# Sixteen transposed tiles instead of fifteen, and single tiles for the signs, in a four-layer graph network

## The chip, the cores and the metric

The kernel runs on one core of one Trainium2 chip. The time is the device time of the whole program in microseconds (us), from one launch. The names of the engines are those of the profile: PE is TensorE (matrix multiplication), DVE is VectorE, ACT is ScalarE, POOL is GpSimd, SP is SyncE, which here only issues DMAs. Each engine works through its own queue of instructions in a fixed order; semaphores hold an instruction back until what it needs is done.

## The reference

Sixteen graphs of 1024 nodes with 64 features each go through four layers. The adjacency matrix is symmetric in its pattern, but not in its values; about one entry in 128 is above zero, and the diagonal is. Each layer adds to `x` a function of `h = max(layernorm(x), 0)`.

```python
# layer 0
x = x + einsum('bnf,of->bno', einsum('bnm,bmf->bnf', adj, h), W0)
# layer 1: messages, and a GRU cell
m = relu(relu(h @ W1 + b1) @ W2 + b2)
msg = relu(einsum('bij,bjh->bih', adj, m))
r, z, n = gates(msg, h)                     # sigmoid, sigmoid, tanh
x = x + (1 - z) * n + z * h
# layer 2: Chebyshev, T0 = h, T1 = adj h, T2 = 2 adj T1 - T0
x = x + (K0 * T0 + K1 * T1 + K2 * T2) @ Wc + bc
# layer 3: quantiles over the neighbours that are left
nb = (adj > 0) without the diagonal; m = row count of nb
removed = every ceil(m / 2)-th neighbour of rows with m > 10, and its mirror image
agg = 0.25 * q25 + 0.5 * q50 + 0.25 * q75   # per node and feature, over self and neighbours
x = x + (relu((h + agg) @ M1 + c1) @ M2 + c2) * mask
```

So the adjacency matrix is multiplied four times per graph (once in layer 0, once in layer 1, twice in layer 2), and layer 3 needs a list of each node's neighbours and a sort of their features.

## The kernel before

**Tiles.** A graph's adjacency matrix is read as eight blocks of 128 columns (512 KB each, `block`, two buffers). PE transposes a block in eight pieces of 128x128, ACT copies the result from two PSUM banks into one tile `AT` of 128x1024 in fp32. There are `AT = 15` such tiles (line 106, taken into stock at line 602), eight for each graph. All four passes over the matrix of one graph read the same eight tiles, and the last pass of layer 2 gives tile after tile back (`into(..., last=True)` in `layers`), provided that the signs of this tile have been taken (`self.masked[b] > j`).

**Chains.** The work is written as Python generators that yield one operation at a time, or the name of a stock from which they want a buffer, or a condition to wait for. `transposing` loads and transposes blocks, graph after graph; it loads the block after the present one before it asks for the present one's `AT` tile. `layering` exists twice, for even and for odd graphs, and runs layers 0 to 2 (`layers`) for each, then the norm in front of layer 3; it ends with two stores by SP into DRAM, `table` (what is gathered) and `rows`. A graph's `X` (two buffers) may be loaded when the graph before has finished the matrix pass of layer 0 (`self.turns`), and its `pay` tile (three buffers) is taken at the end of layer 2. `coding` takes the signs of the transposed tiles, clears the diagonal and multiplies by a table of powers of two, so that sixty-three numbers per node (`words`, then `code`) tell which columns are set. `listing` turns a code into 24 column numbers per node, with DVE's largest-eight operations. `gathering` issues indirect DMAs from POOL, 80 for each graph (ten neighbours for eight tiles of nodes), and, after all graphs, 122 for nodes with more neighbours, which `longest` has picked out. `quantiling` sorts and weighs the gathered rows on DVE (`G`, two buffers, and `net`), and `dense` does the last two matrix products and stores the output.

**Order.** The class `Weave` plans the order of all engines' queues. It holds estimates of each operation's time and of each buffer's readiness, and always issues the operation that can start earliest by these estimates; among those within 0.1 us of each other on one engine it takes the lowest key. A graph's layers, transposes and codes have the key b − 3, its list b − 2, its quantiles and gathers b + 1. The written order is then fixed: on the chip an engine waits for the instruction at the head of its queue. All operations made through these chains have line 303 in the profile, so they are told apart by their tiles. Gathers are line 634, the stores of table, rows and output line 640.

**Around the change.** In `coding` (lines 664 to 694) two tiles of signs are held in one `there` tile of 128x2x1024 in fp16; there are two of these pairs. For each pair ACT takes two signs, DVE clears both diagonal blocks in one multiplication of 128x256, and PE does four multiplications, two for each tile. The result is scaled by ACT into the fp32 tile `words`, which has its own place, and is transposed by PE in four pieces.

Of the kernel before, what the change touches and what calls it, by code (L numbers as in the profile page):

```python
# [10 lines left out]
F32 = mybir.dt.float32  # L11
F16 = mybir.dt.float16
# [4 lines left out]
AF = mybir.ActivationFunctionType  # L17
# [5 lines left out]
P = 128  # L23
N = 1024
NT = N // P
C = 64
NB = 64
S = N // NB
# [74 lines left out]
RANK = 3.0  # L103
SHARE = 3
LONGEST = 512
AT = 15
XTILES = 2
PAYS = 3
LIST_KEY = -2
# [4 lines left out]
UNIT = 2.0 ** -10  # L114
# [213 lines left out]
class Weave:  # L328
# [13 lines left out]
    def stock(self, name, tiles):  # L342
        self.stocks[name] = list(tiles)

    def give(self, name, t):
        self.stocks[name].append(t)
# [121 lines left out]
class Fast:  # L468
# [4 lines left out]
    def __init__(self, tc, half, whole, weights):  # L473
# [107 lines left out]
        def stock(name, count, shape, dtype=F32):  # L581
            weave.stock(name, [p.tile(shape, dtype, name=f"{name}{i}") for i in range(count)])
# [6 lines left out]
        weave.stock("fm", banks[5:8])  # L589


        stock("there", 2, [P, 2, N], F16)
        stock("code", 1, [P, NT, NB])
        self.words = p.tile([P, 512], F32, name="words")
        self.top = p.tile([P, NT, WORDS], F32, name="top")
        self.cand = p.tile([P, NT, CAND], F16, name="cand")
        stock("L", 3, [P, NT, LIST], F16)
# [3 lines left out]
        stock("block", 2, [P, NT, P])  # L601
        stock("AT", AT, [P, N])
        stock("X", XTILES, [P, NT, C])
# [60 lines left out]
    def coding(self):  # L664

        V, T, S = self.V, self.T, self.S
        for b in range(GRAPHS):
            yield float(b) + CODE_KEY
            yield lambda: self.turns > 0
            bank = yield "bits"  # L670
            turned = self.turned[b]
            for j in range(0, NT, 2):
                there = yield "there"
                for i in range(2):
                    yield lambda: len(turned) > j + i
                    yield S.activation(there[:, i, :], turned[j + i], AF.Sign)
                self.masked[b] = j + 2
                own = there.rearrange("p i (t m) -> p (i t) m", m=P)[:, j:j + NT + 2:NT + 1, :]
                yield V.tensor_mul(own, own, self.noteye[:, None, :].to_broadcast([P, 2, P]))
                for i in range(2):  # L680
                    for half in range(2):
                        yield T.matmul(bank[half * NB:(half + 1) * NB, :], self.bits[:, (j + i) * NB:(j + i + 1) * NB],
                                       there[:, i, 512 * half:512 * half + 512], start=j + i == 0, stop=j + i == NT - 1)
                self.weave.give("there", there)
            yield S.activation(self.words, bank, AF.Identity, bias=self.low, scale=1.0 / UNIT)
            self.weave.give("bits", bank)
            bank = yield "tp"
            for q in range(4):
                yield T.transpose(bank[:, q * P:(q + 1) * P], self.words[:, q * P:(q + 1) * P], self.ident)
            code = yield "code"  # L690
            yield S.activation(code.rearrange("p (h q) w -> p q h w", h=2),
                               bank.rearrange("p (q h w) -> p q h w", h=2, w=NB), AF.Copy)
            self.weave.give("tp", bank)
            self.coded[b] = code
# [95 lines left out]
    def longest(self):  # L790
# [5 lines left out]
        for _ in range(3):  # L796
            tiles.append((yield "AT"))
        run = tiles[0][:, 0:BINS * Q]
# [59 lines left out]
        for t in tiled:  # L858
            self.weave.give("AT", t)


    def transposing(self, adj):
# [17 lines left out]
        for i in range(total):  # L880
# [4 lines left out]
            block = blocks.pop(i)  # L885
            at = yield "AT"
            for half in range(2):
# [39 lines left out]
    def layers(self, w, b, x):  # L927
# [9 lines left out]
        def into(bank, h, last=False):  # L937

            def step(j):
# [6 lines left out]
                if last:  # L946
                    yield lambda: self.masked[b] > j
                    give("AT", turned[j])
            return step
# [575 lines left out]
def general_layers(tc, b, x, adj, nodemask, VT, mB, X, H, maskT, c16, ident, ones16, ones_row, eps,  # L1525
# [3 lines left out]
    with tc.tile_pool(name="g1", bufs=1) as p1, tc.tile_pool(name="g2", bufs=2) as p2, \  # L1529
# [16 lines left out]
        def neighbours(g):  # L1546
            AT = p2.tile([P, NT, N], F32, name="AT")
            CN = p1.tile([P, NT, N], F16, name="CN")
# [434 lines left out]
```

## Time and profile before

| what | us |
|---|---|
| median of 13 runs | 2131.77 (2121.52 to 2144.62) |
| the profiled execution | 2133.97 |
| its span, from the first to the last instruction | 2132.0 |
| DVE busy | 1632.6 |
| PE busy | 1523.4 |
| POOL busy | 1432.9 |
| ACT busy | 1073.9 |
| granted clock of PE, mean over the span | 0.787 |

A line of the timeline gives the start in us from the span's start, the length in us, the engine, the line in the code, the operation with its tiles (out<-in) and form, how many of one kind are merged in the line (x), and in brackets how long the engine had been idle before and what ended this. A line of waits gives the waiting engine and tile, then what ended the wait, the sum in us, how often, and the longest. A line of the tile view gives the shortest, median and longest duration in ns, and the start of the first and of the last one in us. Idle time of an engine is a loss only where something later waits for it.

### The profile page before, as it was taken

The page shows a single profiled execution, that of the slowest core. Times are in us where ns is not written, and L with a number is a line of the kernel's source. Part 1 is how long each engine was busy: PE and PEld are TensorE (multiplying, and loading weights), DVE is VectorE, ACT ScalarE, POOL GpSimd, SP SyncE. Part 2 cuts the span into 40 slices and gives each one's busy share as a digit, 9 for nine tenths or more (in the row PEclk, how much of TensorE's full clock was granted, in tenths as well). Part 3 has the DMA queues.
Part 4 walks back from the last instruction along what each step waited for, and adds up shares of the span by engine and source line. Part 5 has one row for each costly group of instructions (what it writes and reads, how often), then busy time and mean ns, then how long its engine had stood idle before and what let it go on. Part 6 is the DMA issues. An engine that isn't in the chain of part 4 may idle for free. (4 is left out here: it accounts for less than half of the span.)

```text
span 2132.0 us, 22993 instructions
## 1 busy us (share of the span) xinstructions
PE 1523.4 (71%) x6172; PEld 713.3 (33%) x6172; DVE 1632.6 (77%) x4293; ACT 1073.9 (50%) x2921; POOL 1432.9 (67%) x1441
## 2 busy tenths in 40 slices
PE   6978677869787888788887878787978873233303
PEld 2443424333433343343433333334343331111202
DVE  2651587977788888888887969797788899949646
ACT  3654646556665657475656474747466532011000
POOL 2047776777576767677777667676757777776772
PEclk9979697978889787879796979787779886555555
DMA  4242626253525353434343353525252314121110
GB/s 122 70 86 57 117 36 96 61 96 61 92 61 88 68 75 80 66 89 62 84 67 89 49 94 61 106 51 95 51 92 51 43 31 42 30 32 23 32 27 11
DMA packets 246840, 140.93 MB, mean 66 GB/s; under 512 B 76048, under 2 KB 223952, under 8 KB 246704
## 3 DMA queue, kind: packets, MB, share of 16 engines
q1 hardware_dynamic: 195664, 88.11, 18.9%
q0 software_dynamic: 46096, 48.62, 17.3%
q10 hardware_dynamic: 4944, 2.66, 0.5%
q8 instruction: 53, 0.87, 0.2%
q14 instruction: 83, 0.68, 0.1%
HBM read 120.10 MB, written 19.17 MB: 65 GB/s over the span
## 5 line engine op out<-in xcount | busy, mean ns | idle before, releaser
L634 POOL DMA_INDIRECT G<-table,pay x1402 | 1403.2, 1001 | 652.8 <-issue 353.7
L303 PE MATMUL bank<-AT,nodes 128*64 128x512 f32 x2048 | 604.2, 669 | 87.1 <-ACT nodes L303 77.2
L303 PEld LDWEIGHTS bank<-AT,nodes 128*64 128x64 f32 x2048 | 181.2, 153 | 383.8 <-issue 221.7
L303 PE MATMUL bank<-G,c 128*128 128x512 f32 (+3 forms) x382 | 172.1, 589 | 184.8 <-DVE G L303 180.0
L303 PE MATMUL bank<-c,block 128*128 128x128 f32 x976 | 223.2, 349 | 102.2 <-DMA block<-in_adj 59.3
L303 ACT ACTIVATE AT<-bank 128x512 f32<-128x512 f32 x256 | 149.6, 589 | 187.2 <-PE bank L303 184.7
L303 PEld LDWEIGHTS bank<-c,block 128*128 128x128 f32 x976 | 147.8, 176 | 227.1 <-issue 143.4
L303 DVE TENSOR_TENSOR G<-G 128x512 f32<-128x512 f32 (+3 forms) x313 | 200.1, 673 | 2.8
L303 ACT ACTIVATE nodes<-X,off,ri 128x64 f32<-128x64 f32 x360 | 141.1, 429 | 45.9 <-DVE off L303 44.6
L303 DVE TENSOR_TENSOR net<-G 128x512 f32<-128x512 f32 (+6 forms) x240 | 150.6, 671 | 11.1 <-ACT G L303 9.1
L303 PEld LDWEIGHTS bank<-G,c 128*128 128x128 f32 x382 | 71.5, 224 | 255.8 <-DVE G L303 128.8
L303 ACT ACTIVATE G<-G,coef 128x64 f32<-128x64 f32 x384 | 98.2, 336 | 110.0 <-DVE coef L303 109.9
L303 ACT ACTIVATE sq<-X,st 128x64 f32<-128x64 f32 x360 | 124.6, 346 | 49.7 <-DVE st L303 33.4
L303 ACT ACTIVATE there<-AT 128x1024 f16<-128x1024 f32 x128 | 132.1, 1050 | 0.9
L303 ACT ACTIVATE wide<-bank 64x512 f32<-64x512 f32 x128 | 75.0, 586 | 109.3 <-PE bank L303 108.1
L303 DVE TENSOR_TENSOR G<-net 128x512 f32<-128x512 f32 (+7 forms) x189 | 117.1, 665 | 0.7
L303 DVE TENSOR_TENSOR G<-G,net 128x512 f32<-128x512 f32 (+3 forms) x177 | 111.3, 678 | 0.9
L303 DVE SCALAR_TENSOR_TENSOR G<-bad,G 128x512 f32<-128x512 f32 (+1 forms) x176 | 109.8, 692 | 0.0
L303 PE MATMUL bank<-wide,wg 64*64 64x512 f32 (+1 forms) x192 | 107.5, 642 | 0.9 <-ACT wide L303 0.4
L303 DVE TENSOR_REDUCE st<-X 128x8 f32<-128x512 f32 x48 | 32.9, 686 | 86.6 <-DMA X<-in_x 85.5
L303 DVE MAX8 L<-cand 128x8 f16<-128x103 f16 x384 | 91.9, 263 | 8.8
L303 PE MATMUL bank<-there,c 128*64 128x512 f16 x256 | 80.3, 450 | 25.4 <-DVE there L303 25.3
(200 smaller groups left out, 2225.8 us busy)
## 6 DMA issues: line engine op xcount, KB each, us to landing
block<-in_adj SPq DMA_DIRECT2D x121, 512.0 KB, 4.2
G<-table,pay POOLq DMA_INDIRECT x1402
rows<-pay SPq DMA_DIRECT2D x16, 632.0 KB, 10.4
table<-pay SPq DMA_DIRECT2D x16, 264.0 KB, 5.3
X<-in_x SPq DMA_DIRECT2D x16, 256.0 KB, 9.6
out<-yo SPq DMA_DIRECT2D x16, 256.0 KB, 2.6
G<-in_adj SPq DMA_DIRECT2D x3, 512.0 KB, 11.0
G<-in_adj ACTq DMA_DIRECT2D x3, 512.0 KB, 9.8
```

The costliest lines, as they stand in the source:

```text
L303: return Op(self, lambda: f(*args, **kwargs), writes, reads, cost, later)
L634: return self.nc.gpsimd.indirect_dma_start(out=out, out_offset=None, in_=table, in_offset=bass.IndirectOffsetOnAxis(ap=at, axis=0))
```

## The change

There are sixteen `AT` tiles. To make room, `there` becomes three single tiles of 128x1024 in place of two pairs, and the separate tile `words` goes: its values are written into a `there` tile, seen as 128x512 in fp32. The loop in `coding` runs over single tiles: one sign, one multiplication of 128x128 that clears the diagonal block, two matrix multiplications. `self.masked` counts tile by tile. In bytes per partition: one `AT` tile more is 4096, `there` goes from 8192 to 6144, and `words` gave 2048.

```diff
-AT = 15
+AT = 16
...
-        stock("there", 2, [P, 2, N], F16)
+        stock("there", 3, [P, N], F16)
         stock("code", 1, [P, NT, NB])
-        self.words = p.tile([P, 512], F32, name="words")
...
-            for j in range(0, NT, 2):
+            for j in range(NT):
                 there = yield "there"
-                for i in range(2):
-                    yield lambda: len(turned) > j + i
-                    yield S.activation(there[:, i, :], turned[j + i], AF.Sign)
-                self.masked[b] = j + 2
-                own = there.rearrange("p i (t m) -> p (i t) m", m=P)[:, j:j + NT + 2:NT + 1, :]
-                yield V.tensor_mul(own, own, self.noteye[:, None, :].to_broadcast([P, 2, P]))
-                for i in range(2):
-                    for half in range(2):
-                        yield T.matmul(bank[half * NB:(half + 1) * NB, :], self.bits[:, (j + i) * NB:(j + i + 1) * NB],
-                                       there[:, i, 512 * half:512 * half + 512], start=j + i == 0, stop=j + i == NT - 1)
+                yield lambda: len(turned) > j
+                yield S.activation(there, turned[j], AF.Sign)
+                self.masked[b] = j + 1
+                own = there[:, j * P:(j + 1) * P]
+                yield V.tensor_mul(own, own, self.noteye)
+                for half in range(2):
+                    yield T.matmul(bank[half * NB:(half + 1) * NB, :], self.bits[:, j * NB:(j + 1) * NB],
+                                   there[:, 512 * half:512 * half + 512], start=j == 0, stop=j == NT - 1)
                 self.weave.give("there", there)
-            yield S.activation(self.words, bank, AF.Identity, bias=self.low, scale=1.0 / UNIT)
+            there = yield "there"
+            words = there.bitcast(F32)
+            yield S.activation(words, bank, AF.Identity, bias=self.low, scale=1.0 / UNIT)
             self.weave.give("bits", bank)
             bank = yield "tp"
             for q in range(4):
-                yield T.transpose(bank[:, q * P:(q + 1) * P], self.words[:, q * P:(q + 1) * P], self.ident)
+                yield T.transpose(bank[:, q * P:(q + 1) * P], words[:, q * P:(q + 1) * P], self.ident)
+            self.weave.give("there", there)
```

## The prediction

> **What bounds the kernel now.** I read the page first, then one tile's instructions (the stores of the table), then what each engine waited for, and last the timelines of ACT, PE, DVE, SP and POOL around one turn of the steady state, 560 to 690 us, where graph 5 ends and graph 6 is under way. The run behind the profile took 2133.97 us, 1.97 more than its span; the median of the runs shown is 2131.77, so the sum below is made against 2134 and taken down by 2.2 at the end.
>
> ```profile
> span 2132.0 us, 22993 instructions
> PE 1523.4 (71%) x6172; PEld 713.3 (33%) x6172; DVE 1632.6 (77%) x4293; ACT 1073.9 (50%) x2921; POOL 1432.9 (67%) x1441
> ```
>
> No engine is full over the span. The steady part is a chain of sixteen graphs, and its step is read from the table stores, one per graph; what POOL (which gathers, and whose last gathers set the end) waits for is the second view.
>
> ```profile
> L640 SPq DMA_DIRECT2D table<-pay x16: 359/366/367, 125.1 to 1770.9; - x16
> ...
> POOL G L634 <- DVE whole L303: 37.9, 5, 13.9
> POOL G L634 <- DMA table<-pay: 31.9, 6, 13.9
> POOL G L634 <- DVE below L303: 19.8, 2, 14.2
> POOL G L634 <- DVE st L303: 8.2, 1, 8.2
> ```
>
> Fifteen steps in 1645.8 us are 109.7 us a graph. The four lines add to 97.8 us. They stand at the starts of graphs' gathers, and the names whole, below and st are only what ended last: each time the gather starts about 6 us after that graph's table store (563.14 and 569.58, 672.94 and 679.56 below). So POOL is short of work by 6.5 us per graph on the mean. Its sixteen stretches of 80 gathers, cut out of the timeline, are 1674 us in sum, 104.6 each: that is the floor under the step if the stores came early.
>
> What makes the store late is seen in one turn. Two chains of layers are in flight, one for even and one for odd graphs, and graph 6 cannot finish layer 0 without its eighth transposed tile.
>
> ```profile
> 623.73 0.58 ACT L303 ACTIVATE AT<-bank 128x512 f32<-128x512 f32 x1
> ...
> 656.09 0.60 ACT L303 ACTIVATE AT<-bank 128x512 f32<-128x512 f32 x1 [9.99 <-PE bank L303]
> ```
> ```profile
> 563.14 0.37 SPq L640 DMA_DIRECT2D table<-pay  x1
> ...
> 672.94 0.37 SPq L640 DMA_DIRECT2D table<-pay  x1
> ...
> 673.99 1.01 SPq L303 DMA_DIRECT2D X<-in_x  x1
> ```
> ```profile
> 569.58 0.94 POOL L634 DMA_INDIRECT G<-table,pay  x1 [14.23 <-DVE below L303]
> ...
> 679.56 0.94 POOL L634 DMA_INDIRECT G<-table,pay  x1 [5.52 <-DVE below L303]
> ```
> ```profile
> 655.99 1.07 PE L303 MATMUL bank<-AT,nodes 128*64 128x512 f32 x2
> ...
> 672.88 2.00 PE L303 MATMUL bank<-w0t,wide 64*128 64x64 f32 x16
> ```
> ```profile
> 676.01 0.67 DVE L303 TENSOR_TENSOR X<-X,bank 128x512 f32<-128x512 f32 x1
> ...
> 684.03 0.69 DVE L303 TENSOR_REDUCE st<-X 128x8 f32<-128x512 f32 x1 [5.24 <-DMA X<-in_x]
> ```
>
> Seven tiles of graph 6 are turned by 624.3; the eighth starts at 656.1, when graph 5's last pass gives its first tile back: fifteen tiles are eight for graph 5 and seven for graph 6. Its block had been asked for at 621.9, in the same timeline of SP. From 656.1 to the sum of layer 0 (676.7) are 20.6 us, and these lie behind graph 5's last pass and in front of graph 6's layer 1. The step is therefore a closed loop: last pass of one graph, eighth tile, layer 0's end, then layers 1 and 2 up to the next last pass. That it is latency and not load shows between the first two stores (125 to 224 us, 99.0 us), where DVE is busy for 37.6 and PE for 74.6.
>
> **The change, part by part.** *The sixteenth tile.* It takes the eighth tile out of the loop: graph 6's could be turned 31.8 us earlier (656.1 less 624.3) and its layer 1 may start while graph 5 is in layer 2. Tiles are then wanted again only by graph 7's first transposes, which have a whole step. Nothing is added: the same 1024 transposes, 256 copies and block loads, moved earlier. Past SP: the eighth load of a graph and, because a graph's X may be asked for once the one before has finished layer 0, the X load can be queued in front of the table store, not behind it; its issue is 1.0 us in the row above, which the store may bear once a graph (15 us in all at most, and less than nothing if X lands earlier). Past POOL nothing moves: it issues gathers in graph order alone.
>
> What is late next. POOL allows 104.6 a graph. DVE is busy 91.5, 92.0, 93.2 and 90.5 us in the four steps from 563 to 1001 (mean 91.8), and in a step of the same length it waits some 16 us: over 673 to 1673, nine graphs, 48.1 us for X, 27.6 for the root of the norm, 24.0 for the candidates' relu, that is 11.1 a graph, and about 5 a graph for smaller waits. With the 0.8 us below, 91.8 + 0.8 + 11.1 is 103.7, under POOL's floor; with the smaller waits kept it is 108.7. The second graph in layer 1 gives DVE and PE other work in front of these waits, but each queue runs in one written order and the waits of a chain do not vanish. I take the middle of POOL's floor and that sum, (104.6 + 108.7) / 2 = 106.7, as nothing in the trace says which is nearer: 3.0 us a graph, 15 times, **−45 us**. Ends: −97.8 (all of POOL's waits at starts go) and 0 or worse (the third case below).
>
> *The first graph.* Graph 0's last passes, 99 to 125 us, now share PE and ACT with graph 1's eighth tile and layer 1. Eight transposes of 0.33 us and two copies of 0.6 are 3.8 us in front of the first store: **+4 us**, since POOL's row begins there. Bounds: nothing if they fall into the 25 us of PE's idle time of that stage, 12 if one pass of graph 1's layer 1 goes first as well (8.29 us for the 32 instructions in the timeline at 708).
>
> *Signs one by one.* The activations stay 128 of 1050 ns. The masking multiply is done 128 times over 128 columns, not 64 times over 256 (287 ns). The new size has no row; 192 columns take 258 and 72 take 235, so I take 245: 8 x 0.245 less 4 x 0.287 is 0.8 us of DVE a graph, 13 us in all, with 0.7 and 0.9 as ends from those rows. It is hidden in DVE's 16 us of waits a graph; were that cover gone, it would be 13 us on the end. A sign's order is finer: behind it on ACT are copies and relus, and the multiply now comes one sign (1.05 us) earlier for the first of each pair; gain or loss at most that per pair, off the loop, because the list it feeds is wanted some 50 us later. With three singles a sign waits for the multiplication three signs back (two pairs: the third or fourth back). In the trace ACT is idle for 0.9 us in front of all 128 signs, so a buffer wait costs nothing now, and nothing up to 1 us each on ACT's 42 us of idle time.
>
> The VectorE: DVE Perf Modes page of the Trainium skill (§ Rules for kernel authors) says to keep the number of operations small, and its errata section puts some 150 cycles on each one whatever its size. By that estimate the 64 added multiplies cost 64 x 0.156 us, 10 us, all of it against the change; the rows above give a little more.
>
> *Words in a `there` tile.* The activation (680 ns) and four transposes stay. They hold one of three tiles for about 4 us (663.35 to 664.75 in this turn at the least), after the graph's last sign, and the next graph's first sign comes 10 us or more later: nothing, and 16 x 4 us at worst on a chain with 50 us to spare.
>
> Sum: 2134 − 45 + 4 = 2093, less 2.2, and I say **2091 us**.
>
> **The rivals.** *Nothing to gain.* The loop is cut, but the step stays with DVE's order: 91.8 + 0.8 busy and its waits as they are make 108.7 to 109.7. Or graph 1's X tile (two of them) or the pay tile (three) takes the wait over: a pay tile comes back with its graph's output store (630.79 in this turn, for graph 2) and graph 5's is taken at 658.0, so that there are 27 us of room, a little less than the 31.8 the loop gives. For it: DVE is over 82% busy in each steady step. Against: the step of 99 us without DVE load. Price: 0 to 1 us a graph, 2117 to 2136.
>
> *Slower.* Two graphs in layers at once fill DVE's queue with two sets of short dependent operations (norms of 0.17 to 0.7 us, each with a wait on ACT in the middle). The order is written by a planner whose times are estimates: X's load lands after 9.6 us by the profile, where DVE stands waiting today. If such waits come to stand in front of the other graph's final norm, they are on the way to the store. Place: DVE between two stores. It decides at 109.7 − 92.6 = 17.1 us of DVE waiting a graph, against 16 now; at 20 us the step is 112.6, +2.9, and 15 steps give +44: 2176. For it: margin is one microsecond. Against: DVE would have more work ready to stand in front of a wait, not less.
>
> *The change does not do what it says.* The eighth block may not be there, or the order may put its transposes behind layer 2 all the same. The block is asked for at 621.9 and PE waits 5 us at 630 to 635, so little speaks for it; it would give 2132 and up to 13 for the multiplies. I count it with the first rival.
>
> **How the numbers follow.** The forecast gets 0.55, nothing to gain 0.15, slower 0.30. A difference of 0.3%, about 6.4 us, is what a measurement of this kernel can tell from none. Of the 0.15, 0.05 lies below 2125, 0.08 within and 0.02 above. Faster is 0.60, same 0.08, slower 0.32. The forecast's own range is 2034 (all 97.8 us) to 2120. The whole range goes from 2034 to 2160: below it are waits that I don't see, above it the slower case's far half; together 2 in 10.
>
> The SBUF — State Buffer page of the Trainium skill (§ Who interferes with whom) states that a DVE operation with two SBUF inputs can hold up a GpSimd one that reads SBUF. The 64 added multiplies are such operations; if each held a gather for its own length, an estimate by that page is 64 x 0.245, 16 us more on POOL. The trace's gathers have a median of 944 ns beside a mean of 1001, which shows that some are held, not by whom.
>
> **What would show it.** In the changed profile: graph b+1's sixteenth copy no longer waits for graph b's last pass, and its layer-0 sum is done 20 us or more before graph b's store. POOL's waits at the starts fall from 97.8 us to about 50, the stores' step to 106.7, and the first store is at 129. The `there` multiply has 128 instructions near 245 ns. The prediction is wrong if the step stays at 109 or more: then DVE's waits per graph will be 16 us or more, and that row tells the first rival from the second. The tail after graph 15's gathers should keep its length, 237 us from 1895 to 2132; if it grows, the lists or the quantiles are behind POOL there.

## The result: 2.1% slower, and the profile after

The changed kernel takes 2178.01 us (median of 14 runs, 2159.6 to 2192.2) against 2130.86 us before (62 runs beside it, 2119.9 to 2146.3): 1.021 of the time, 95% interval 1.019 to 1.0231. (This and the ratios below are those on record, which go by the fast runs alone; quotients of the two medians differ from them by up to 0.2%.) The forecast was 2091 us with a range up to 2160. Both missed, and the sign was wrong.

The page of the changed kernel, its head:

```profile
span 2181.0 us, 23079 instructions
PE 1548.0 (71%) x6172; PEld 715.7 (33%) x6172; DVE 1635.8 (75%) x4357; ACT 1079.3 (49%) x2921; POOL 1425.8 (65%) x1441
```

The 64 added multiplies raised DVE's busy time by 3.2 us only, and POOL and ACT do what they did. The span is 49 us longer all the same, so the time is in waits. The span falls into four pieces, read from POOL's timeline: the time up to the first gather, the sixteen stretches in which a graph is gathered, the idle time between two stretches, and the tail behind graph 15's last gather.

| us | before | after | difference |
|---|---|---|---|
| up to the first gather | 130.4 | 139.8 | +9.4 |
| sixteen stretches | 1666.3 | 1698.6 | +32.3 |
| between them | 98.0 | 105.9 | +7.9 |
| tail | 237.3 | 236.7 | −0.6 |
| span | 2132.0 | 2181.0 | +49.0 |

The largest piece is the one that the prediction had treated as a fixed floor. The table's stores and POOL's waits after the change (a group row of the stores, then engine, tile, what the wait ended on, us in all, times, longest):

```profile
L639 SPq DMA_DIRECT2D table<-pay x16: 359/366/367, 134.3 to 1806.2; - x16
...
POOL G L633 <- DMA table<-pay: 123.1, 1, 123.1
POOL G L633 <- DVE net L303: 59.9, 3, 28.8
POOL G L633 <- PE bank L303: 59.8, 42, 17.4
```

Two of these waits as they were before:

```profile
POOL G L634 <- PE bank L303: 12.1, 30, 3.2
...
POOL G L634 <- DVE net L303: 9.9, 1, 9.9
```

(The 123.1 us are the wait in front of the very first gather.) The stores' step is (1806.2 − 134.3) / 15 = 111.5 us, 1.8 longer than before. "DVE net" has gone from 9.9 to 59.9 us and "PE bank" from 12.1 to 59.8. (Of the 59.9, 50.7 are two waits in front of graphs 7 and 14; the third, like the 9.9 before, lies in the tail.) Both are waits for a gather buffer G: net is the sorting network that reads G, and the bank is filled from G by the last matmuls that use it. Inside stretches POOL stood idle for 40.7 us (waits above 1 us, less the usual 0.3), against 2.2 before. The wait for a graph's own store is no longer the only one.

The turn that the prediction looked at, graph 6's layer 0, in the changed kernel. Timelines of ACT, SP, PE and DVE:

```profile
592.00 0.58 ACT L303 ACTIVATE AT<-bank 128x512 f32<-128x512 f32 x1
...
630.67 0.59 ACT L303 ACTIVATE AT<-bank 128x512 f32<-128x512 f32 x1
...
677.33 0.60 ACT L303 ACTIVATE AT<-bank 128x512 f32<-128x512 f32 x1 [0.39 <-PE bank L303]
```
```profile
576.96 0.37 SPq L639 DMA_DIRECT2D table<-pay  x1
...
687.38 0.37 SPq L639 DMA_DIRECT2D table<-pay  x1
```
```profile
582.36 0.42 PE L303 MATMUL bank<-c,nodes 128*64 128x128 f32 x1 [15.14 <-ACT nodes L303]
...
666.68 3.65 PE L303 MATMUL bank<-AT,nodes 128*64 128x512 f32 x16 [0.26 <-DVE nodes L303]
...
672.81 0.66 PE L303 MATMUL bank<-c,block 128*128 128x128 f32 x4
```
```profile
698.15 0.67 DVE L303 TENSOR_TENSOR X<-X,bank 128x512 f32<-128x512 f32 x1
```

With sixteen tiles the eighth need not wait for graph 5's last pass. In this turn it comes behind it all the same: the second half of that pass ends on PE at 670.3, the eighth tile's transposes start at 672.8, and its copies are at 673.5 and 677.3, 10 us before graph 5's store at 687.4 (15 us before). The other tiles are late as well. Six copies, three tiles, are done by 592.6; then none comes for 38 us, and the sum of layer 0 ends at 698.8, 11.4 us after graph 5's store, where before it was 3.8 us after the store. The written order has put the transposes of graph 6 behind other work (PE does graph 5's layers and the last products of a quantile from 594 to 629), and PE stood still for 15.1 us around the start of that turn.

This turn is the worst of fifteen. Before, the sixteenth copy of the next graph starts 11.3 to 12.0 us after the first operand of a graph's last pass is ready, in every turn; after the change it starts 11 to 27 us ahead of that in eleven turns and 4 to 15 behind it in four. So the tile does come earlier in most. But the sum of layer 0 does not follow: on the mean of the fifteen turns it ends 4.3 us behind the previous graph's store before and 3.6 after, and from the sixteenth copy to the matmuls of this sum (graphs 4 to 14) it takes 12 to 17 us before and 17 to 47 after.

### The profile page after: what moved, and what is told of

It reads as the page before. It is cut to its first block, busy times and chain, and to the rows that moved or that the text cites. A ratio compares the mean times of both kernels' runs of the same rounds, so it can differ in the third digit from the quotient of the medians.

```text
span 2181.0 us, 23079 instructions
## 1 busy us (share of the span) xinstructions
PE 1548.0 (71%) x6172; PEld 715.7 (33%) x6172; DVE 1635.8 (75%) x4357; ACT 1079.3 (49%) x2921; POOL 1425.8 (65%) x1441
## 5 line engine op out<-in xcount | busy, mean ns | idle before, releaser
L303 PE MATMUL bank<-AT,nodes 128*64 128x512 f32 x2048 | 592.7, 662 | 49.0 <-ACT nodes L303 37.3
L303 PE MATMUL bank<-G,c 128*128 128x512 f32 (+3 forms) x382 | 198.6, 651 | 204.3 <-DVE G L303 166.4
L303 PEld LDWEIGHTS bank<-AT,nodes 128*64 128x64 f32 x2048 | 173.5, 150 | 356.0 <-issue 209.4
L303 ACT ACTIVATE there<-AT 128x1024 f16<-128x1024 f32 x128 | 134.3, 1050 | 1.0
L303 PE MATMUL bank<-c,nodes 128*64 128x128 f32 x128 | 50.7, 407 | 90.7 <-ACT nodes L303 89.5
L303 PE MATMUL bank<-wide,wg 64*64 64x512 f32 (+1 forms) x192 | 103.1, 618 | 2.3 <-ACT wide L303 2.1
```

The source lines that it names most:

```text
L303: return Op(self, lambda: f(*args, **kwargs), writes, reads, cost, later)
```

## Experiments

Every batch ran beside the kernel before on the same chip, and chips differ by up to 1%: before took 2130.86 us beside the changed kernel, 2126.82 in the first batch (e1 to e4), 2111.91 in the second (e5 to e8), 2111.55 in the third (e9 to e12), 2110.55 in the fourth (e13 to e16). So ratios are compared. In the table, "inside" is POOL's idle time within stretches, "starts" that in front of them, whether for the store or for G (both less 0.3 us a gather), and "half clock" the sum of those stretches of the trace's clock record that begin between 40 and 1700 us and grant PE half its speed. The last five columns are of one profiled execution each, not divided by the kernel before of the same batch: e5, in the order of before and 1.0005 of its time, has a step of 108.2 us on its chip, against 109.7. A profiled execution can also lie off its median: e2's is the fastest of ten (2109.89 us, median 2128.19), e7's the slowest of ten (2117.4, median 2108.55).

| run | ratio to before, 95% | first store | stores' step | starts | inside | half clock |
|---|---|---|---|---|---|---|
| before | 1 | 125.1 | 109.7 | 93.5 | 2.2 | 570 |
| after | 1.021 (1.019–1.0231) | 134.3 | 111.5 | 101.4 | 40.7 | 659 |
| e1 signs alone | 1.0183 (1.0149–1.0216) | 133.2 | 111.5 | 112.3 | 6.5 | 614 |
| e2 tile alone | 1.0006 (0.997–1.0042) | 125.8 | 108.0 | 47.6 | 18.3 | 539 |
| e3 after, lists later | 1.0157 (1.0122–1.0192) | 133.1 | 110.1 | 43.8 | 56.5 | 597 |
| e4 before, lists later | 1.0059 (1.0028–1.009) | 125.5 | 109.3 | 59.8 | 38.0 | 526 |
| e5 singles, order of before | 1.0005 (0.9981–1.0029) | 126.1 | 108.2 | 76.3 | 0.8 | 567 |
| e6 after, PE filled | 1.010 (1.0055–1.0145) | 126.9 | 108.4 | 62.9 | 31.0 | 430 |
| e7 before, PE filled | 0.9978 (0.9962–0.9994) | 129.4 | 108.3 | 81.6 | 0.7 | 413 |
| e8 tile alone, filled | 0.9966 (0.9931–1.0001) | 124.0 | 106.8 | 35.6 | 16.7 | 389 |
| e9 signs alone, filled | 1.0045 (1.0012–1.0078) | 124.7 | 109.2 | 71.3 | 5.4 | 437 |
| e10 e6 and lists later | 1.0069 (1.0038–1.0099) | 126.4 | 108.8 | 18.6 | 63.0 | 451 |
| e11 e8 filled more | 0.9946 (0.992–0.9972) | 125.7 | 107.5 | 46.3 | 22.4 | 362 |
| e12 e11, lists later | 1.0078 (1.0051–1.0104) | 132.4 | 108.6 | 69.6 | 18.3 | 440 |
| e13 after, lists apart | 0.9976 (0.9955–0.9998) | 133.5 | 107.5 | 56.4 | 5.6 | 536 |
| e14 e13 filled | 0.9896 (0.9864–0.9928) | 129.9 | 107.2 | 48.1 | 9.3 | 429 |
| e15 e11, lists apart | 0.9853 (0.9821–0.9885) | 125.3 | 106.3 | 18.8 | 21.0 | 348 |
| e16 after, start filled | 1.0188 (1.0157–1.022) | 128.6 | 109.8 | 87.7 | 30.6 | 611 |

### Which part of the change costs (e1, e2)

e1 is the change without its first line: single-tile signs, words in one of them, fifteen tiles. Against the changed kernel:

```diff
-AT = 16
+AT = 15
```

> The signs part alone: fifteen transposed tiles, three single tiles of signs, words in one of them. Theory A (what costs is the written order of DVE's queue: a list of neighbours, 80 or more operations and some 30 us, is put inside a quantile, so that the gather buffer G comes back late and POOL stands): in the written order of this kernel a whole list stands inside the quantiles of graphs 5 and 6, where the kernel before has none inside those of graphs 1 to 12 and the changed one has one inside 2, 5, 7 and 12. So two long waits of POOL, 15 to 30 us each, behind graphs 7 and 8, and 2150 to 2165. Theory B (the sixteenth tile costs, by bringing two graphs' layers into each other's way): the time of before plus no more than the 13 us of small multiplies, 2130 to 2145, with no long wait of POOL inside a graph's gathers.

e2 is the first line alone. So that sixteen tiles fit beside the pairs, the words go into a pair of signs and the scratch of the lists into an output tile:

```diff
-AT = 15
+AT = 16
-        self.words = p.tile([P, 512], F32, name="words")
-        self.top = p.tile([P, NT, WORDS], F32, name="top")
+            there = yield "there"
+            words = there[:, 0, :].bitcast(F32)
...
+        lent = yield "yo"
+        top = lent[:, 0:NT * WORDS].rearrange("p (t w) -> p t w", w=WORDS)
```

> The sixteenth tile alone: pairs of signs as before; the room comes from writing words into a pair of signs and the list's scratch tile top into an output tile. Theory A: in the written order a whole list stands inside the quantiles of graphs 2, 4 and 10, so three waits of POOL of 6 to 25 us behind graphs 4, 6 and 12 and 2145 to 2175. Theory B: all of the loss, 2170 to 2185, and spread over all graphs. If the tile takes the eighth transposition out of the loop as I forecast, the time would be below before, 2091.

The signs alone cost 1.8%, the tile alone nothing that can be measured. The prediction had it the other way round: 45 us of gain for the tile, nothing for the signs. In e1 the loss stands mostly at starts: in front of graph 7 alone POOL waits for 36.8 us, until 933.3, 42 us behind that graph's store at 891.2. What ends this wait is "DVE net", with a list inside graph 5's quantile, as Theory A said; e1's 2163.03 us lie in its range.

e2's 2128.19 us lie in none of the three ranges. Lists stand inside the quantiles of graphs 2, 4 and 10, and POOL's waits behind graphs 4, 6 and 12 came as Theory A said (12.2, 16.5 and 10.5 us), all three for G, but the time did not rise. So a list inside a quantile makes POOL wait, but what such a wait costs depends on the rest of the order.

### Lists half a graph later (e3, e4)

```diff
-LIST_KEY = -2
+LIST_KEY = -1.5
```

The key is the priority with which the planner takes up a graph's list. Why lists came under suspicion is seen on DVE in the changed kernel. This is the quantile of graph 5 (hits is its first operation, the operations on G and net its network):

```profile
834.57 0.32 DVE L303 TENSOR_TENSOR hits<-G,pay 128x160 f32<-128x160 f32 x1 [0.21 <-DMA G<-table,pay]
...
881.90 0.42 DVE L303 TENSOR_SCALAR top<-code 128x504 int32<-128x504 int32 x1
...
889.04 0.69 DVE L303 TENSOR_TENSOR G<-net,G 128x512 f32<-128x512 f32 x1
...
903.64 0.67 DVE L303 TENSOR_TENSOR G<-net,G 128x512 f32<-128x512 f32 x1
```
```profile
904.58 0.99 POOL L633 DMA_INDIRECT G<-table,pay  x1 [0.30 <-issue]
927.45 1.15 POOL L633 DMA_INDIRECT G<-table,pay  x1 [21.88 <-DVE net L303]
```

From 881.9 to 910.7 the list of graph 8 runs, and the network gets single operations in between. From the first operation to the last this quantile takes 97 us, where the others of graphs 1 to 11 with less than 4 us of a list inside take 66 to 71. There are two gather buffers; graph 7 needs the one that graph 5's quantile still reads, and POOL stands for 21.9 us, until 20 us behind graph 7's store at 907.4, where some 6 are usual. Before, the quantiles of graphs 1 to 12 hold no list. After, those of 0, 2, 5, 7 and 12 hold 23 to 29 us of DVE's work on one, and the long waits for G are exactly in graphs 2, 4, 7, 9 and 14.

> The changed kernel with one number changed: the key of the lists is b - 1.5, not b - 2, so that the quantile of graph b - 3 goes before the list of graph b where both can start. Theory A: G comes back in time again, POOL's waits of over 5 us inside a graph's gathers go, its waits on DVE net and PE bank (119.7 us in the changed kernel) fall below 40, and the time falls by 50 to 70 us, to 2110 to 2130, at or under the kernel before. Theory B: the layers of two graphs still share the queues, so that not more than 15 us come back: 2163 or more.

> The kernel before (fifteen tiles, pairs) with the same one number changed. Theory A: it has no list in front of a quantile's operations to begin with, so nothing is to be won: 2125 to 2160, as the list now comes later than the eighth tile's wait allows. If the key alone were a gain whatever the number of tiles, it would be 2080 to 2110. Theory B says nothing of it.

The later key helps the changed kernel by half a per cent, far less than expected, and costs the kernel before as much. The traces tell why: with the later key the quantiles of graphs 1 to 13 have a list inside in both kernels, and in the changed kernel the waits at starts fall to 44 and those inside rise to 57. This was the wrong tool for the question, not an answer to it.

### The instructions or their order (e5)

The kernel before, with each pair's two signs in two tiles and its multiply done as two, while the planner goes on reckoning with one of the old cost. So every engine's written order is that of before, one multiply more per pair apart (and a few operations behind the last graph's list).

```diff
-                own = there.rearrange("p i (t m) -> p (i t) m", m=P)[:, j:j + NT + 2:NT + 1, :]
-                yield V.tensor_mul(own, own, self.noteye[:, None, :].to_broadcast([P, 2, P]))
+                yield self.each_own(there, j)
...
+    def each_own(self, there, j):
+        own = [there[i][:, (j + i) * P:(j + i + 1) * P] for i in range(2)]
+        def make():
...
+        return Op(self.V, make, own, own, 0.155 + 2 * P / 960)
```

> The kernel before with each pair of signs put into two separate tiles and the pair's one masking multiply (128x256) done as two (128x128), one behind the other; every engine's written order is otherwise that of before, instruction by instruction, and fifteen transposed tiles are kept. Theory I (the finer instructions themselves cost: 64 more operations on DVE, smaller tiles): most of the 36 us that the single-tile signs cost at fifteen tiles comes back here, 2145 to 2163 us, first store near 133. Theory O (the written order costs, not the instructions): 2121 to 2135 us, first store at 125 as before, DVE's busy time up by 3 to 10 us and hidden in its waits.

The group of multiplies there (min/median/max ns, first and last start):

```profile
L702 DVE TENSOR_TENSOR there<-there,c x128: 204/217/285, 46.9 to 1637.5; 128x128 f16<-128x128 f16 x128
```

1.0005. The same 128 small multiplies that e1 has cost nothing in the order of before. Theory O holds: the 1.8% come with the order that the planner writes once the signs are single. Nor is it a lack of tiles: planned with four single tiles in place of three, the kernel of e1 has the same written order, instruction by instruction.

### PE at half clock (e6 to e9, e16)

What else differs is seen in the first graph. Stretches of the timeline, first before, then after. The columns are the stretch and its length, the busy time and the number of instructions of PE, PEld, DVE, ACT and POOL, then the granted clock, the DMA share and GB/s:

```profile
52.00:56.00 4.00, 4.00 (x16) 2.00 (x15) 2.70 (x6) 4.00 (x7) 0.00 (x0) 0.62 0.44 128
56.00:60.00 4.00, 3.01 (x21) 1.98 (x21) 1.23 (x4) 3.94 (x13) 0.00 (x0) 1.00 0.47 136
60.00:64.00 4.00, 3.96 (x19) 1.71 (x18) 2.69 (x10) 4.00 (x11) 0.00 (x0) 1.00 0.01 2
```
```profile
52.00:56.00 4.00, 1.99 (x9) 0.94 (x10) 3.50 (x9) 3.99 (x9) 0.00 (x0) 0.95 0.59 167
56.00:60.00 4.00, 4.00 (x13) 1.66 (x12) 0.85 (x4) 3.05 (x6) 0.00 (x0) 0.50 0.29 88
60.00:64.00 4.00, 4.00 (x9) 0.91 (x10) 0.00 (x0) 1.67 (x3) 0.00 (x0) 0.50 0.01 2
...
72.00:76.00 4.00, 4.00 (x14) 1.70 (x15) 2.44 (x14) 2.01 (x9) 0.00 (x0) 0.50 0.01 4
```

After the change PE has work for only 2 of the 4 us from 52 on. Then its clock is 0.50 from 55.6 to 76.1, 20.5 us in which PE is busy nearly all the time. Before, the same place has two windows of 3.4 us at half clock (from 51.7 and from 65.3). This goes with the first store's delay, 125.1 to 134.3: e1 and e3, which have the order of the single signs, show the same 20.5 us and 133; e2 and e5, which haven't, show neither. Whether it is the cause, filling PE's idle time tells.

The filling puts matmuls that do no work in front of an operation before which the planner foresees PE idle. They write ones where that operation will overwrite, or add zeros to what is being summed. The order stays as it is, and the planner doesn't reckon with them:

```diff
+IDLE, FILL, WARM = 0.8, 0.7, (5.0, 1720.0)
...
-        line, ins = op.line, op.make()
+        line = op.line
+        gap = start - self.free.get(line, 0.0)
+        if op.fill and self.last.get(line) and gap > IDLE and WARM[0] < start < WARM[1]:
+            each, fill = op.fill
+            for _ in range(min(40, int(FILL * gap / each))):
+                ins = fill()
...
+        ins = op.make()
```

> The changed kernel, every engine's written order kept, with idle stretches of PE that the written order foresees (over 0.8 us) filled to about 70% with matmuls that do no work: they write ones into a region that the next matmul overwrites, or add zeros to one that is being summed. Theory C (PE at half clock is what the new order costs: in the profiles PE ran at half clock for 658 us between 40 and 1700 us in the changed kernel, 614 with the single-tile signs alone, 570 before, 539 with the sixteenth tile alone): half-clock time falls under 500 us and the time by 20 to 45 us against 2178, to 2133 to 2158; the first store comes at 127 or earlier, because the 20 us at half clock from 55 to 76 us go. Theory W (the order's waits on DVE and ACT cost, and the clock only follows): 2170 to 2190, also where the half-clock time falls.

> The kernel before with the same filling of PE's foreseen idle stretches. Theory C: half-clock time between 40 and 1700 us falls from 570 to under 480 us and the time by 10 to 30 us, to 2097 to 2117. Theory W: 2120 to 2140 us, with the filling matmuls in front of real ones costing 0 to 12 us.

> The sixteenth tile alone with signs in pairs (the kernel of the second experiment, 2128 us), with the same filling of PE's foreseen idle stretches. Theory C: 2095 to 2118 us, faster than the kernel before. Theory W: 2122 to 2140.

The same stretches in e6, where PE does 10 instructions more from 52 to 56:

```profile
52.00:56.00 4.00, 2.85 (x19) 1.29 (x19) 3.26 (x9) 3.99 (x9) 0.00 (x0) 1.00 0.57 168
56.00:60.00 4.00, 4.00 (x18) 1.57 (x17) 0.85 (x4) 3.73 (x8) 0.00 (x0) 1.00 0.24 70
60.00:64.00 4.00, 4.00 (x24) 2.35 (x22) 0.81 (x3) 3.73 (x9) 0.00 (x0) 1.00 0.21 63
```

With 812 matmuls that compute nothing the changed kernel loses half of its deficit, 1.021 to 1.010, and its first store comes 7.4 us earlier. The stores' step falls from 111.5 to 108.4; some 1 us of that is the chip's (e5 above). The kernel before gains only 0.2% by the same means, though its half-clock time falls by 157 us (570 to 413), and Theory C's 10 to 30 us did not come there. So time at half clock has no fixed price. It should count where others wait for PE, but beyond the first graph no run shows which stretches these are. e8's interval just touches 1 and is inconclusive by itself.

> The single-tile signs alone at fifteen tiles (1.0183 of before in the first experiment) with PE's foreseen idle stretches filled as in the sixth. If half-clock time is what this part of the change costs, it comes to 0.995 to 1.004 of the kernel before, with the first store at 127 or earlier and the stores' step at 109 or less. If half clock is one part and late networks (a graph's candidate lists written between another graph's gathers and its quantile, so that a gather buffer comes back late) the other, 1.006 to 1.013.

> The changed kernel with PE's foreseen idle stretches filled in the first graph's setup alone, some 100 us from the start. First store at 128 or earlier in place of 134. If the start's 7 us reach the end, 1.0165 to 1.0185 of before; if the later steps take them back, 1.020 to 1.022.

e16 is e6 with the filling cut off after the first graph's setup, `WARM = (5.0, 85.0)`. e9: three quarters of what the single signs cost at fifteen tiles come back (1.0183 to 1.0045), less than clock alone would give and more than the mixed expectation. e16: filling the first graph alone brings its store to 128.6 but the ratio only to 1.0188; the intervals overlap with 1.021, so how much of the start reaches the end stays open. e6's interval lies wholly below e16's, so most of what filling gives comes behind the first graph.

### Both remedies by the key (e10 to e12)

e10 is e6 with the lists' key of e3. e11 is e8 with more filling, and e12 is e11 with another key:

```diff
-IDLE, FILL, WARM = 0.8, 0.7, (5.0, 1720.0)
+IDLE, FILL, WARM = 0.3, 0.9, (5.0, 1720.0)
...
-LIST_KEY = -2
+LIST_KEY = -1.9
```

> The changed kernel with both remedies: PE's foreseen idle stretches filled (1.010 of before by itself) and the lists' key half a graph later (1.0157 by itself, against 1.021 unchanged). If the two causes are separate and add, 1.003 to 1.007 of before. If the later lists only moved the loss to DVE's order, 1.008 to 1.015. If it is clock alone that decides, no different from 1.010 by over 0.3%.

> The sixteenth tile with signs in pairs, filled more: foreseen idle stretches of PE over 0.3 us to 90%, in place of over 0.8 us to 70% (0.9966 of before, interval 0.9931 to 1.0001). If more filling keeps the clock up, half-clock time falls under 388 us and the ratio to 0.985 to 0.994. If filling matmuls begin to stand in front of real ones, 0.997 to 1.005.

> The same with the lists' key a tenth of a graph later (-1.9). If the lists inside quantiles cost what is left of gathers' waits in this kernel (some 40 us at starts, 13 inside), 0.980 to 0.992 of before. If the written order is what matters and its changes are as good as random, 0.990 to 1.015.

e10 ends inside the range for two causes that add, but it gains only 0.3% on e6, with intervals that overlap, and trades waits at starts for waits inside as e3 did; it settles little. e11 is faster than before by 0.5%, just outside the range for more filling, with less time at half clock (362 us); its interval overlaps e8's, so what the fuller filling adds isn't shown. e12 loses that and more: a tenth of a graph in one key moves the time by 1.3%, and its expected gain did not come. Its trace shows why it could not: even this key puts a list inside each quantile of graphs 1 to 13.

### Lists kept out of the quantiles (e13, e14, e15)

One rule for the planner takes away the suspected cause. The planner writes the rest of the order anew as well, which e12 shows can be worth a per cent by itself; so the marks to look at are the waits:

```diff
-            yield from self.lists(b)
+            yield from self.apart(self.lists(b))
...
+            if isinstance(want, Op) and want.line is self.V:
+                yield lambda: not self.sorting
...
+        self.sorting = True
         m1 = small("m1", T)
...
+        self.sorting = False
         self.weave.add(self.dense(c, bufs, net, where), c["key"] - 1.0)
```

> The changed kernel with one rule more for the written order: between a quantile's first operation on DVE and its last network operation no DVE operation of a list is written. Nothing else is asked for. Theory G (lists inside quantiles keep gather buffers, and POOL waits inside a graph's stretch, 41 us in the changed kernel): those waits fall under 8 us and the ratio from 1.021 to between 0.998 and 1.006. Theory C (half clock is the larger part): 1.008 to 1.016, with the first store still near 134 and half-clock time still over 600 us.

> The same with PE's foreseen idle stretches filled as in the sixth experiment. If the clock and the lists inside quantiles together are what the change costs, 0.985 to 1.000 of before. If something of the written order is still missing from the account, 1.003 to 1.012.

> Sixteen tiles with signs in pairs, the lists kept out of quantiles, and the fuller filling of the eleventh experiment (0.9946 of before). If POOL's waits inside stretches (22 us there) go without new ones at the starts, 0.980 to 0.990; if they come back at the starts, 0.992 to 1.002.

POOL's waits in e13, and DVE around the end of graph 5's quantile there:

```profile
POOL G L634 <- DVE cand L303: 18.8, 3, 8.7
...
POOL G L634 <- PE bank L303: 12.1, 30, 3.2
...
POOL G L634 <- DVE net L303: 9.9, 1, 9.9
```
```profile
874.64 0.45 DVE L303 TENSOR_REDUCE coef<-off 128x72 f32<-128x288 f32 x1
...
883.82 0.73 DVE L303 MAX8 more<-code 128x8 f32<-128x63 f32 x5
```

The list now stands behind the quantile's last operation. "DVE net" and "PE bank" are back at 9.9 and 12.1 us, the values of before. The changed kernel with this rule takes 0.9976 of before: the whole loss is gone. Theory G's mark is met (5.6 us inside), its range (0.998 to 1.006) missed by a hair on the good side; of Theory C's marks only the first store came, at 133.5. Divided as above, e13's span of 2101.7 is 138.6 + 1664.8 + 60.9 + 237.4. Against the changed kernel the stretches lose 33.8 us and the time between them 45.0. About 20 us of this sum are the chip's and not the rule's: before took 2110.55 us here and 2130.86 beside the changed kernel. e5, in the order of before on a chip where before took 2111.91, has 1660.5 in stretches and 80.9 between them, against 1666.3 and 98.0, so the chip's part lies mostly between them.

The two causes are not independent: half-clock time fell from 659 to 536 us without a single filling matmul. Why is not shown: it may be that gathers on time bring PE its work on time, or only that the order is another. But they are not one cause either. e14 adds the filling and comes to 0.9896. That is better than both kernels, with the change in it. The fastest is e15, sixteen tiles with paired signs and both remedies: 2078.2 us against 2110.55, 0.9853. The expected number came, by another way than expected: the waits inside stretches stay at 21 us, now small waits for earlier gathers to land, and those at starts fall from 46 to 19. Its page:

```profile
span 2077.0 us, 25206 instructions
PE 1562.4 (75%) x7288; PEld 749.5 (36%) x7288; DVE 1629.3 (78%) x4293; ACT 1073.6 (52%) x2921; POOL 1431.3 (69%) x1441
```

PE issues 1116 matmuls more than before (7288 against 6172).

### What stays open (e17, e18)

e17 is the kernel before with both remedies, e18 the changed kernel with both and the fuller filling. They were to tell whether e15's gain is the sixteenth tile's, set free, or the remedies' own.

> The kernel before, fifteen tiles and pairs, with the two remedies that gave 0.9853 at sixteen tiles: lists kept out of quantiles, PE's foreseen idle stretches filled more. If the gain of that kernel is the remedies' and the sixteenth tile adds nothing, 0.983 to 0.989 here too. If the sixteenth tile is worth what the prediction gave it, some 1 to 2% once nothing else is late, 0.994 to 1.000 here.

> The changed kernel itself, sixteen tiles and single-tile signs, with both remedies, the filling as full as in the fifteenth experiment. If single tiles cost nothing of their own, 0.982 to 0.988 of before, as with pairs (0.9853). If they still cost by the order that comes with them, 0.988 to 0.996.

Nothing follows from them. In that batch the kernel before itself took 3290.7 us (11 runs), e17 3421.05 (1.0407 of it) and e18 3380.55 (1.0286). In e17's timeline PE stands still for 63 us with nothing that the profile shows to wait for:

```profile
418.51 0.42 PE L305 MATMUL bank<-c,nodes 128*64 128x128 f32 x1 [63.03 <-issue]
```

The instructions last as long as elsewhere (a gather 0.95 us); the time lies between them. As the kernel before, unchanged, took half as long again, this is a disturbance from outside the kernels, whose source the profiles don't show, and the ratios can't stand beside the others. What speaks for the tile: fifteen tiles with the first filling give 0.9978, and of lists inside quantiles before had next to none (2.2 us of waits inside), so the rule has little to take away there. That is argued, not shown.

## Why the prediction was wrong, point by point

*"It takes the eighth tile out of the loop" and the 3.0 us a graph, −45 us: this step failed.* The tile did take away the wait for graph 5's last pass. But the step assumed the rest of the order as it was, so that layer 0's sum would come with the tile, 20 us or more before the store. The planner writes the order anew and does other things first: layer 0's sum ends 3.6 us behind the previous store on the mean, against 4.3 before, and in e2, with the tile alone, 4.6. In four turns of fifteen, graph 6's among them, the last copies come in the last pass or behind it all the same; this is the rival *The change does not do what it says*, for which the prediction saw little. Alone the tile is worth 1.0006. In the profiled execution of e2 the stores' step is 108.0, and the waits at starts fall from 93.5 to 47.6 us, of which 16.1 come back inside stretches; but that execution is 18 us under its median. What holds the sum of layer 0 behind the store once the tile is there, no run shows.

*"POOL allows 104.6 a graph", the floor: this step failed with it.* "What is late next" was looked for on DVE in front of the store alone. It was the gather buffer, held by a quantile with a list in it. Inside a stretch POOL had waited 2.2 us in the whole run before, and the prediction took that as given; it became 40.7. (The figure itself is a little high: taken from the first gather's start to the last one's end, the sixteen stretches are 1666.3 us, 104.1 each; windows of whole us gave 1674.)

*"Signs one by one", 0.8 us a graph, hidden: right as to the instructions, wrong as to the step.* A small multiply takes 219 ns (I took 245), and their starts overlap with their neighbours', so that DVE's busy time rose by 3.2 us and not 13. e5 shows that they cost nothing in the order of before. The sentence that failed is that the finer order is a "gain or loss at most that per pair, off the loop": it led to another written order on PE, DVE and ACT, worth +1.8%. By the fixed cost per operation on the VectorE: DVE Perf Modes page of the Trainium skill, the estimate was 10 us. Counted one by one the trace agrees (the multiplies take 18.3 us in all before and 28.7 after); of busy time it is 3.2, as the records overlap.

*Words in a `there` tile: nothing.* No wait for it was seen.

*"+4" for the first graph, bounds 0 to 12: the size (+9.2) lies inside, the mechanism was another.* The prediction blamed graph 1's tile and layer 1. e2 has these and its first store is at 125.8. Most of it is PE's clock in the order that comes with the single signs: with this order and PE filled, the first store is at 126.9 (e6) and 124.7 (e9).

*The rival "Slower", 2176 us: the right number by half of the right path.* Its sign was DVE waiting more than 17.1 us between two stores; it is 17.8 on the mean of nine graphs (16.3 before), so it was rightly given as the point to watch. But its price counted 2.9 us a graph on the store, and the store's step grew by 1.8. The span's 49 us are 26 in these steps, 9 in front of the first store, and 14 behind the last one, where graph 14's gathers had waited 28.8 us for G. And the waits it named (norms of two graphs in each other's way) are not what has to go: e13 keeps both graphs in their layers, and DVE's waits fall to 14.3 us a graph once the lists stand elsewhere.

*The SBUF — State Buffer page's 16 us on POOL* did not come: the gather's median is 944 ns before and after, and in e5, with all 64 added multiplies, the sixteen stretches are 1660.5 us in sum, against 1666.3.

*Right:* the tail keeps its length (236.7 against 237.3), and the mark by which the forecast was to be called wrong, a step of 109 or more, is the one that shows it.

## What to carry to other kernels

Where a planner writes the order, a change of buffers or of one operation's size is a change of the whole order. Cost it from what the new order may put between a producer and the buffer it has to give back, and expect a change of time from the order alone; here it was 1 to 2%. Test order and instructions apart, by giving the new instructions the old order. And look at the clock row where an engine's work comes in pieces: here 2 us of idle time were followed by 20.5 us of work at half clock.

## What the runs showed of the hardware

PE's clock goes by windows. Every stretch at half clock in the trace's clock record is a whole multiple of 3.41 us long. I divided the time from 40 to 1750 us into these windows and set PE's busy share in each beside the clock of the next. From full clock, every window that was less than 40% busy was followed by one at half clock, 33 of 33 before and 27 of 27 after; windows at least 90% busy were so in 7 of 440. Between 40 and 90% it went either way, full clock in most; the window in front of the 20.5 us at 55.6 was 53% busy. The way back is harder: at half clock no window under 70% busy was followed by full clock (0 of 121), and of those at least 90% busy 111 of 199 were followed by another at half clock. The two outer rules hold without exception in e1 to e16 too: 452 of 452 windows under 40% busy, and 0 of 854 under 70%. (Busy is what the profile models as busy.)

The TensorE: Matmul & The Clock Gate page of the Trainium skill (Part 1, on the clock gate) names a window of about 3.4 us, half clock after an idle one and full clock after a busy one. The window and the two clocks agree with the trace. But a window needn't be idle to cost the clock, and one busy window often doesn't bring it back: 20.5 us after the change, at 55.6.

What I had not expected is how cheap the remedy is. 812 matmuls of no use took 229 us off the time at half clock (659 to 430) and 1.1% off the changed kernel. In the kernel before the same filling took 157 us off it and 0.2% off the time.
